# A four-layer graph network on one core: the change of layers in a written order, third passes two banks behind, projection pairs spread, longer first fills

## The chip, the cores and the metric

The kernel runs on one core of a Trainium2 chip. Times are device microseconds of one execution. A core has TensorE (PE in the profile, its weight loads apart as PEld), VectorE (DVE), ScalarE (ACT), GpSimd (POOL) and SyncE (SP), which here issues DMAs only. Each engine runs its own instructions in order and waits on semaphores for the others. The measure is the median of the runs, lower is better.

## The reference

The inputs are 1024 nodes of 512 features, 16384 edges, and a condition tensor of 16 batches of 256 rows by 512.

```python
def _attn(xf, cond, Wq, Wk, Wv, Wo):
    xb = xf.reshape(BS, n // BS, d)                      # 16 batches of 64 nodes
    q = (xb @ Wq).reshape(BS, -1, H, DH)                 # 8 heads of 64
    k = (cond @ Wk).reshape(BS, -1, H, DH)
    v = (cond @ Wv).reshape(BS, -1, H, DH)
    att = jnp.einsum('bnhd,bmhd->bhnm', q, k) * DH ** (-0.5)
    w = jax.nn.softmax(att, axis=-1)
    o = jnp.einsum('bhnm,bmhd->bnhd', w, v).reshape(BS, -1, H * DH)
    return (o @ Wo).reshape(n, d)
...
x_in = h_in
h = batch_norm(x_in)
h = _gcn(h, src, dst, gcn_in_w, gcn_in_b, n)             # normalised neighbour sums
for i in range(4):
    a = _attn(_ln(h, ln2_w[i], ln2_b[i]), cond, Wq[i], Wk[i], Wv[i], Wo[i])
    h = h + a
    u = _ln(h, ln3_w[i], ln3_b[i]) @ geglu_w[i] + geglu_b[i]
    val, gate = jnp.split(u, 2, axis=-1)
    h = h + (val * gelu(gate)) @ ffo_w[i] + ffo_b[i]
h = _gcn(h, src, dst, gcn_out_w, gcn_out_b, n)
return x + h + x_in                                       # x_in is relu(layernorm(x))
```

## The kernel before

The nodes are held as eight blocks of 128 rows (`h[0]` to `h[7]`, parts of the tile `hall`). All of the kernel is one traced function; a scheduler then orders each engine's instructions by dependencies and by the order of the trace, except where the code fixes it: `pin` chains PE's instructions in written order, `issue_after` holds an instruction behind another, `waiting_for` does so across engines. PSUM has eight banks of 128 x 512, all of one ring (`bank`), and large SBUF tiles come from a ring of 36 `slots`.

**The start.** The batch norm, the projection into the first graph step (`hw_in`) and the counting of edges (`cs`) come first; `begin` (L682) fills PE's pauses there with parts of layer 0's keys and values in plain float32 (one unit of eight matmuls of 128x512 records): `k0` while the batch norm's shift is awaited, `v0` after the counts, `k1` while the degrees' inverse root is worked out. Then the first aggregation runs over the blocks (`agg_in`), then layer 0's layer norm, keys, values and queries.

**Keys and values.** `Twelve` (L341) is one unit, a 128 x 512 output in one bank from operands split into twelve-bit parts: `begin` multiplies the high parts, then the low parts (four matmuls each, in the float form fp32r), and asks ACT to scale the bank (L359); `end` adds the third pass, sums times sums, and copies the bank out (ACT L366 for even units, DVE L364 for odd). The parts of the condition are `ah_c` (ACT L299), `al_c` (DVE L300), `as_c` (POOL L302); those of the weights `bh`, `bl`, `bs` (L310 to L320). For the value weights, `bs_wv` is made by ACT and POOL through an extra tile (`room`), for the key weights by DVE. `steps_of` runs units one behind the other: the third pass of a unit follows the first two of the next.

**The rounds.** In each layer, `g` runs over eight blocks (two batches each). Round `g` of 0 to 6 does: scores (`sc`, PE), softmax (maximum on DVE L810, exponentials on ACT L815, division on DVE L820), the four key units of block `g + 1`, transposes of the probabilities (`tr_pr`) and their product with the values (`po`, in `mix`), the four value units of block `g + 1`, and for odd `g` the output projection of two blocks (`attn_out_pair`, L895) as seven quarter products in two banks `oab` and `ocd`, with sums on POOL (`pair_sums`). The condition of block `g + 2` is split meanwhile (`split_cond`).

**The feed-forward** follows with gated quarters (`Quad`, `Gated`) and the products of `ffn_out` (L1182), in four banks `fa` to `fd`, whose results DVE adds into `kept` and `hall`.

**The change of layers** (L1680 to L1692, and the head of the next layer, L1381 to L1399): the last two `ffn_out` of a layer, each for half of the blocks; the split of the next layer's key weights, condition and value weights; sums of the query weights on POOL; the layer norm of each half (moments and a root by small DVE operations, `less`, the scaling of four blocks on ACT L1318), the transposes (`tr_ln`) with scaling into `ln2T`, and then keys and values of block 0, and queries (`qa` and so on). The first half's transposes come ahead of the keys.

## Time and profile before

| | |
|---|---|
| median of three runs | 2480.94 us (2479.92 to 2481.77) |
| profiled execution | 2480.42 us |
| its span | 2478.6 us |
| granted TensorE clock, mean | 0.991 |

The profile gives for each engine its busy time; a busy PE is one with a matmul in flight. Of ACT's work in the whole span, 112.1 us are gate functions, 118.1 us exponentials and some 146 us the scalings of key and value banks; POOL's largest group is `as_c`:

```profile
L302 POOL TENSOR_TENSOR as_c<-ah_c,al_c 128x512 fp32r<-128x512 f32 x128 | 189.3, 1506 | 543.8 <-DVE al_c L300 490.3
L1094 ACT ACTIVATE g<-g 128x512 f32<-128x512 f32 x192 | 112.1, 584 | 280.8 <-PE g L1080 278.5
L359 ACT ACTIVATE v<-v 128x512 f32<-128x512 f32 x127 | 73.9, 582 | 222.4 <-PE v L348 222.4
L359 ACT ACTIVATE k<-k 128x512 f32<-128x512 f32 x126 | 72.6, 590 | 141.0 <-PE k L348 141.0
L815 ACT ACTIVATE pr<-sc,nmax 128x256 f32<-128x256 f32 x256 | 118.1, 478 | 76.7 <-DVE nmax L810 76.6
```

A row of groups reads: line, engine, operation, what it writes from what, shapes, count | busy us, mean ns of one | idle us of the engine just before these, and what ended most of it. A row of the waits reads: engine, what waited, what it waited for: us in total, times, longest. A row of the timeline reads: start, us, engine, line, operation, count, and in brackets the engine's idle time before it with its releaser.

### The profile page before, as it was taken

The page shows a single profiled execution, that of the slowest core. Times are in us where ns is not written, and L with a number is a line of the kernel's source. Part 1 is how long each engine was busy: PE and PEld are TensorE (multiplying, and loading weights), DVE is VectorE, ACT ScalarE, POOL GpSimd, SP SyncE. Part 2 cuts the span into 40 slices and gives each one's busy share as a digit, 9 for nine tenths or more (in the row PEclk, how much of TensorE's full clock was granted, in tenths as well). Part 3 has the DMA queues.
Part 4 walks back from the last instruction along what each step waited for, and adds up shares of the span by engine and source line. Part 5 has one row for each costly group of instructions (what it writes and reads, how often), then busy time and mean ns, then how long its engine had stood idle before and what let it go on. Part 6 is the DMA issues. An engine that isn't in the chain of part 4 may idle for free. (4 is left out here: it accounts for less than half of the span.)

```text
span 2478.6 us, 33729 instructions
## 1 busy us (share of the span) xinstructions
PE 2384.1 (96%) x12532; PEld 1775.7 (72%) x12532; DVE 1586.5 (64%) x3053; ACT 998.1 (40%) x2023; POOL 949.6 (38%) x851
## 2 busy tenths in 40 slices
PE   8999999999989999999989999999989999999999
PEld 4667786577867777477766777577766777667787
DVE  9764455787675445777784444777785444678764
ACT  7434454343334445443333444533334444434320
POOL 0133222665332224455532223446532322366531
PEclk9999999999999999999999999999999999999999
DMA  6042120111301101011202111021121111011140
GB/s 195 21 134 82 47 86 18 43 43 51 107 20 54 56 18 52 22 56 48 90 29 65 47 35 35 18 60 52 43 90 47 47 40 47 18 43 43 51 145 35
DMA packets 108843, 138.31 MB, mean 56 GB/s; under 512 B 8232, under 2 KB 65904, under 8 KB 108672
## 3 DMA queue, kind: packets, MB, share of 16 engines
q1 hardware_dynamic: 106576, 130.64, 16.6%
q0 software_dynamic: 1376, 4.30, 0.5%
q8 instruction: 104, 1.70, 0.3%
q10 hardware_dynamic: 720, 1.11, 0.1%
q14 instruction: 67, 0.55, 0.1%
HBM read 119.25 MB, written 16.78 MB: 55 GB/s over the span
## 5 line engine op out<-in xcount | busy, mean ns | idle before, releaser
L302 POOL TENSOR_TENSOR as_c<-ah_c,al_c 128x512 fp32r<-128x512 f32 x128 | 189.3, 1506 | 543.8 <-DVE al_c L300 490.3
L1094 ACT ACTIVATE g<-g 128x512 f32<-128x512 f32 x192 | 112.1, 584 | 280.8 <-PE g L1080 278.5
L1031 POOL TENSOR_TENSOR gsa<-gha,gla 128x512 fp32r<-128x512 f32 x96 | 126.1, 1336 | 103.5 <-DVE gla L1028 103.5
L359 ACT ACTIVATE v<-v 128x512 f32<-128x512 f32 x127 | 73.9, 582 | 222.4 <-PE v L348 222.4
L348 PE MATMUL k<-as_c,bs_wk 128*128 128x512 f32 x504 | 141.8, 404 | 18.1 <-ACT k L359 18.1
L1031 POOL TENSOR_TENSOR gsb<-ghb,glb 128x512 fp32r<-128x512 f32 x48 | 70.0, 1458 | 219.4 <-DVE glb L1028 219.4
L815 ACT ACTIVATE pr<-sc,nmax 128x256 f32<-128x256 f32 x256 | 118.1, 478 | 76.7 <-DVE nmax L810 76.6
L348 PE MATMUL v<-bh_wv,ah_c 128*128 128x512 f32 x508 | 145.6, 408 | 0.0
L364 DVE COPY v<-v 128x512 f32<-128x512 f32 x62 | 42.3, 681 | 153.0 <-PE v L348 153.0
L348 PE MATMUL v<-bs_wv,as_c 128*128 128x512 f32 x508 | 139.8, 397 | 0.0
L348 PE MATMUL k<-ah_c,bh_wk 128*128 128x512 f32 x504 | 139.1, 399 | 0.0
L1195 PE MATMUL fa<-wff,fT 128*128 128x256 f32 x512 | 124.2, 385 | 13.6 <-DVE kept L1205 13.6
L1080 PE MATMUL g<-gr,gsa 128*128 128x512 f32 x384 | 136.6, 437 | 0.0
L348 PE MATMUL k<-al_c,bl_wk 128*128 128x512 f32 x504 | 136.5, 393 | 0.0
L348 PE MATMUL v<-bl_wv,al_c 128*128 128x512 f32 x508 | 136.3, 390 | 0.0
L1107 ACT ACTIVATE g<-g,gcols 128x512 f32<-128x512 f32 x96 | 67.5, 703 | 164.5 <-DVE g L1115 161.3
L359 ACT ACTIVATE k<-k 128x512 f32<-128x512 f32 x126 | 72.6, 590 | 141.0 <-PE k L348 141.0
L348 PEld LDWEIGHTS k<-as_c,bs_wk 128*128 128x128 f32 x504 | 90.2, 189 | 45.9 <-ACT k L359 13.3
L1080 PE MATMUL g<-gr,gha 128*128 128x512 f32 x384 | 122.8, 401 | 0.0
L1195 PEld LDWEIGHTS fa<-wff,fT 128*128 128x128 f32 x512 | 97.1, 191 | 35.2 <-DVE kept L1205 18.0
L1080 PE MATMUL g<-gl,gla 128*128 128x512 f32 x384 | 118.6, 390 | 0.0
L348 PEld LDWEIGHTS v<-bs_wv,as_c 128*128 128x128 f32 x508 | 92.9, 188 | 28.7 <-issue 9.2
(368 smaller groups left out, 5868.7 us busy)
## 6 DMA issues: line engine op xcount, KB each, us to landing
ct<-cond_dram SPq DMA_DIRECT2D x48, 512.0 KB, 4.5
wff<-in_L_gnn_ffo_w_dram SPq DMA_DIRECT2D x32, 512.0 KB, 4.5
gxb<-in_L_gnn_geglu_w_dram SPq DMA_DIRECT2D x96, 128.0 KB, 2.2
gxa<-in_L_gnn_geglu_w_dram SPq DMA_DIRECT2D x96, 128.0 KB, 2.4
cond<-in_L_gnn_cond_dram SPq DMA_DIRECT2D x32, 256.0 KB, 3.7
cond_dram<-ct SPq DMA_DIRECT2D x16, 512.0 KB, 3.7
wk<-in_L_gnn_Wk_dram SPq DMA_DIRECT2D x8, 512.0 KB, 6.1
wv<-in_L_gnn_Wv_dram SPq DMA_DIRECT2D x8, 512.0 KB, 8.4
```

The source lines that it names most:

```text
L302: nc.gpsimd.tensor_tensor(twelve_bits(s)[:, k, :], h[:, k, :], l[:, k, :], OP.subtract)
L348: pin(nc.tensor.matmul(self.bank, twelve_bits(left[k // 2])[:, k % 2, self.c * P:(self.c + 1) * P], twelve_bits(right[k // 2])[:, k % 2, : ...
L359: nc.scalar.mul(self.bank, self.bank, 1.0 + TINY)
L364: nc.vector.tensor_copy(self.to, self.bank)
L815: nc.scalar.activation(pr3[:, a, :], ps3[:, a, :], AF.Exp, bias=nmax[:, a:a + 1], accum_out=tot[:, a:a + 1])
L1031: pin(nc.gpsimd.tensor_tensor(s_at, h_at, l_at, OP.subtract))
L1080: pin(nc.tensor.matmul(to, self.part(i, which)[:, k, :], self.rights[i][which].bitcast(F32R)[:, k, :], start=start and k == 0, stop=stop a ...
L1094: pin(nc.scalar.mul(to, to, 1.0 + TINY))
L1107: pin(nc.scalar.activation(to, of, AF.Gelu, bias=gcols[:, cg:cg + 1]))
L1195: each(nc.tensor.matmul(to[:, q * M:(q + 1) * M], left[i][k][:, (2 * s + q) * P:(2 * s + q + 1) * P], right[i][:, k, :], start=start and q ...
```

## The change

- `staggered` takes the place of `steps_of`, and `keys` and `values` return lists of units. In the rounds, a key unit's third pass comes two units behind instead of one: k0, k1, k2, third of k0, k3, third of k1, third of k2, first transposes, third of k3.
- In a pair, quarter product 5 precedes 4; the third pass of the third value unit stands between the second and third part of the pair; the last product of a pair goes behind the next round's scores, except at `g` = 5. For odd `g`, the split of the condition goes behind the pair's sums. One layer norm of blocks moves from `g` = 5 to `g` = 6.
- At a change of layers PE's and DVE's orders are written out (`pin`, and the new `in_order`, which chains DVE's instructions in the order of the trace). The splits of weights and condition, the moments and the roots stand at chosen places of the two `ffn_out`. The transposes of the first half come behind the first two passes of the first value unit and the last key unit's third pass, those of the second half behind the last value unit. The sums of the value weights move to DVE, the query-weight sums behind the second `less`.
- At the start, two plain key units are made ahead of `hw_in`, the plain value unit is cut in two around the degrees, and layer 0 begins with keys ahead of transposes.

The core of the diff:

```diff
+    @contextmanager
+    def in_order(engine):
+        traced = nc.cur_bb.bb.instructions
+        n = len(traced)
+        before = next((i for i in reversed(traced) if i.engine == engine), None)
+        yield
+        for i in traced[n:]:
+            if i.engine == engine:
+                if before is not None:
+                    tc.add_manual_dep(i, before.name, mybir.DependencyInfo(
+                        mybir.DependencyClass.NoSync, mybir.DependencyReason.DATA))
+                before = i
...
-    def plain(to, left, c, right):
-        for k in range(KC):
+    def plain(to, left, c, right, of=range(KC)):
+        for k in of:
             nc.tensor.matmul(to, left[k // 2][:, k % 2, c * P:(c + 1) * P],
...
-    def steps_of(units):
-        before = None
-        for u in units:
+    def staggered(units, beside):
+        for i, u in enumerate(units):
             u.begin()
-            if before:
-                before.end()
-            before = u
-            yield
-        before.end()
-    def keys(l, g, wk, begun=None):
+            if i:
+                units[i - 1].end()
+            if i in beside:
+                beside[i]()
+        units[-1].end()
+    def keys(l, g, wk, begun=None, n=0):
         kTs[g] = begun or slots_of(2, f"kT_{l}_{g}")
-        return steps_of([Twelve(f"k_{l}_{g}_{c}", wk, c, conds[g], kTs[g][c // 2][:, c % 2, :], c % 2)
-                         for c in range(1 if begun else 0, KC)])
-    def values(l, g, wv, begun=None):
+        return [Twelve(f"k_{l}_{g}_{c}", wk, c, conds[g], kTs[g][c // 2][:, c % 2, :], c % 2)
+                for c in range(n, KC)]
+    def values(l, g, wv, begun=None, n=0):
         vs[g] = begun or slots_of(2, f"v_{l}_{g}")
-        return steps_of([Twelve(f"v_{l}_{g}_{c}", conds[g], c, wv, vs[g][c // 2][:, c % 2, :], c % 2)
-                         for c in range(1 if begun else 0, 2 * MB)])
+        return [Twelve(f"v_{l}_{g}_{c}", conds[g], c, wv, vs[g][c // 2][:, c % 2, :], c % 2)
+                for c in range(n, 2 * MB)]
...
     with tc.issue_after(shifted_last.ins):
-        begin("k0", raw_wk, raw_x[0, 0])
+        for c in range(2):
+            begin("k0", c, raw_wk, raw_x[0, 0])
...
-        begin("v0", raw_x[0, 0], raw_wv)
+        first_v = bank("begun_v0")
+        plain(first_v, raw_x[0, 0], 0, raw_wv, range(2))
         with tc.issue_after(load_dve.ins):
             for j in counted:
                 if j % 2:
                     degrees(j // 2, C[j // 2], t512(f"part_{j // 2}"))
+        with tc.issue_after(degrees.last.ins):
+            plain(first_v, raw_x[0, 0], 0, raw_wv, range(2, KC))
+        nc.scalar.copy(begun["v0"][0][:, 0, :], first_v)
...
-        product(4, d, False)
-        nc.vector.tensor_tensor(h22, d, h22, OP.add)
         product(5, b, False)
         nc.vector.tensor_tensor(u2, b, p1, OP.add)
         t.tensor_tensor(p7, p7, u2, OP.add)
+        product(4, d, False)
+        nc.vector.tensor_tensor(h22, d, h22, OP.add)
         t.tensor_tensor(h22, p7, h22, OP.add)
...
         if r:
             each(nc.vector.tensor_tensor(u, a, u, OP.add))
+            for do in beside[2:]:
+                do()
         else:
             nc.scalar.copy(u, a)
         product(6, c, True)
...
-        for do in beside[1:]:
+        for do in beside[1:2]:
...
+    mv_ready = {}
+    def take_moments(l, blocks):
+        n = len(blocks)
+        mv = mv_ready[blocks[0]] = small.tile([P, 2 * n], F32, tag=f"mv{n}", name=f"mv_{l}_{blocks[0]}",
+                                              bufs=2)
+        moments_into(mv, [h[nb] for nb in blocks], f"ln2_{l}_{blocks[0]}")
     def ready_first(l, blocks):
-        name = f"ln2_{l}_{blocks[0]}"
-        scaled_by_act(blocks, *moments([h[nb] for nb in blocks], name), name)
+        mv, name = mv_ready.pop(blocks[0]), f"ln2_{l}_{blocks[0]}"
+        scaled_by_act(blocks, mv, deviations(mv, name), name)
...
-    with waiting_for(scale_first.last, mybir.EngineType.Pool):
-        wq = load_w(Wq[0], "wq_0")
-        ffb = load_row(ffo_b, 0, "ffb_0")
-        wq = weight_sums(wq, "wqs_0")
+    wq = load_w(Wq[0], "wq_0")
+    ffb = load_row(ffo_b, 0, "ffb_0")
...
         if l:
-            flow = keys(l, 0, wk)
-            for _ in range(4):
-                next(flow)
-            then = values(l, 0, wv)
-            next(then)
-            next(flow, None)
-            ready_first(l, left_to_turn[2:])
+            units = keys(l, 0, wk) + values(l, 0, wv)
+            to_turn = [0, 1, 4, 5], [2, 3, 6, 7]
+        else:
+            scale_first(1, deviations(mv_first[1], "ln2_0_4"))
+            with waiting_for(scale_first.last, mybir.EngineType.Pool):
+                wq = weight_sums(wq, "wqs_0")
+            units = keys(0, 0, wk, begun["k0"], 2) + values(0, 0, wv, begun["v0"], 1)
+            to_turn = [0, 1, 2, 3], [4, 5, 6, 7]
+        def turn_some():
+            turn_first(l, to_turn[0])
+            if l:
+                sum_first(nc.gpsimd, 0)
+                sum_first(nc.gpsimd, 1)
+        staggered(units, {4 if l else 2: turn_some, len(units) - 1: lambda: turn_first(l, to_turn[1])})
+        if not l:
             sum_first(nc.gpsimd, 0)
             sum_first(nc.gpsimd, 1)
-            for _ in range(3):
-                next(then)
-            turn_first(l, left_to_turn)
-            sum_first(nc.vector, 2)
-            sum_first(nc.vector, 3)
-            next(then, None)
-        else:
-            scale_first(1, deviations(mv_first[1], "ln2_0_4"))
-            turn_first(0, [0, 1, 2, 3])
-            for _ in keys(0, 0, wk, begun["k0"]):
-                pass
-            turn_first(0, [4, 5, 6, 7])
-            for nb in range(2):
-                sum_first(nc.gpsimd, nb)
-            for nb in range(2, 4):
-                sum_first(nc.vector, nb)
-            for _ in values(0, 0, wv, begun["v0"]):
-                pass
             fetch_cond(2)
+        sum_first(nc.vector, 2)
+        sum_first(nc.vector, 3)
...
-        oTs, flow = [], None
+        oTs, ends = [], []
         for g in range(NG - 1):
             if g == NG - 2:
                 take_ln3()
                 raw = load_geglu(l, 0)
             probs = scores(l, g, qT, kTs.pop(g))
-            if flow:
-                next(flow, None)
+            for end in ends:
+                end()
+            if g == NG - 2:
+                ln3_norm(g - 2, g - 1)
...
-            flow = keys(l, g + 1, wk, begun.pop("k1") if l == 0 and g == 0 else None)
-            for _ in range(4):
-                next(flow, None)
-            then = values(l, g + 1, wv)
-            oTs.append(mix(l, g, probs, vs.pop(g), (lambda: next(flow, None), nothing,
-                                                    lambda: next(then))))
-            flow = then
+            k = keys(l, g + 1, wk, *((begun["k1"], 1) if l == 0 and g == 0 else ()))
+            for i, u in enumerate(k):
+                u.begin()
+                if i > 1:
+                    k[i - 2].end()
+            k[-2].end()
+            v = values(l, g + 1, wv)
+            oTs.append(mix(l, g, probs, vs.pop(g), (k[-1].end, nothing, v[0].begin)))
...
-            split_cond(l, g + 2)
+            with tc.issue_after(pair_sums.last.ins) if g % 2 else nullcontext():
+                split_cond(l, g + 2)
             if l:
                 load_cond(l, g + 3)
-            next(flow)
-            next(flow)
+            v[1].begin()
+            v[0].end()
+            v[2].begin()
+            v[1].end()
             if g % 2:
                 pair = attn_out_pair(g - 1, *blocks, wo7, bank(f"oab_{l}_{g}"), bank(f"ocd_{l}_{g}"),
                                      pin)
...
                                  f"ln3_{l}_{g - 3}")
             if g == NG - 2:
                 for nb in range(4):
-                    ln3_turn(nb)
-            next(flow)
+                    ln3_turn(nb, each=pin)
+            v[3].begin()
             if g % 2:
-                for _ in pair:
-                    pass
-            if g == NG - 3:
-                scale_kept()
-                ln3_norm(g - 1, g)
+                next(pair)
+            v[2].end()
+            ends = [v[3].end]
+            if g % 2:
+                next(pair)
+                if g == NG - 3:
+                    next(pair, None)
+                    scale_kept()
+                else:
+                    ends.insert(0, lambda pair=pair: next(pair, None))
             if g == NG - 2:
                 for nb in range(4, 6):
-                    ln3_turn(nb)
+                    ln3_turn(nb, each=pin)
                 for nb in (g - 2, g - 1):
                     ln3_sums(nc.gpsimd, nb)
...
-            ffn_out(l, R - 1, 0, fT, wff, kept)
-            wk = right_parts(raw_wk, f"wk_{l + 1}")
-            with waiting_for(Gated.last, mybir.EngineType.Pool):
+            wk, wv = [[], [], []], [[], [], []]
+            def split(to, raw, name, *of):
+                for i in of:
+                    for part, t in zip(to, right_parts(raw[i:i + 1], f"{name}_{l + 1}_{i}")):
+                        part.extend(t)
+            half = [0, 1, 4, 5], [2, 3, 6, 7]
+            with in_order(mybir.EngineType.DVE):
+                ffn_out(l, R - 1, 0, fT, wff, kept, pin, (lambda: split(wk, raw_wk, "wk", 0),
+                                                          lambda: split(wk, raw_wk, "wk", 1)))
+                take_moments(l + 1, half[0])
+                ffn_out(l, R - 1, 1, fT, wff, kept, pin, (lambda: split_cond(l + 1, 0),
+                                                          lambda: split(wv, raw_wv, "wv", 0, 1),
+                                                          lambda: ready_first(l + 1, half[0])))
+                take_moments(l + 1, half[1])
+                ready_first(l + 1, half[1])
+            with waiting_for(scaled_by_act.last, mybir.EngineType.Pool):
                 wq = weight_sums(wq, f"wqs_{l + 1}")
-            ready_first(l + 1, [0, 1, 4, 5])
-            split_cond(l + 1, 0)
-            ffn_out(l, R - 1, 1, fT, wff, kept)
-            wv = right_parts(raw_wv, f"wv_{l + 1}", acc_tile)
-            turn_first(l + 1, [0, 1, 4, 5])
-            left_to_turn = [2, 3, 6, 7]
-            ready_first(l + 1, left_to_turn[:2])
```

More of the change, by code (lines that the diff above doesn't have):

```diff
@@ L306, in right_parts @@
     def right_parts(x, name, room=None):
-        parts = [slots_of(2, f"{n}_{name}") for n in ("bh", "bl", "bs")]
+        parts = [slots_of(len(x), f"{n}_{name}") for n in ("bh", "bl", "bs")]
         for i, (h, l, s, x) in enumerate(zip(*parts, x)):
@@ L561, in degrees @@
         nc.vector.tensor_tensor(of_d, part[:, :P], part[:, P:2 * P], OP.add)
-        nc.tensor.matmul(pdeg[:, d:d + 1], of_d, ones, start=True, stop=True,
-                         skip_group_check=True)
+        degrees.last = nc.tensor.matmul(pdeg[:, d:d + 1], of_d, ones, start=True, stop=True,
+                                        skip_group_check=True)
     def low_hot(t, name):
@@ L680, in gnn_kernel, with begin @@
     begun = {n: slots_of(2, f"{n}_begun") for n in ("k0", "v0", "k1")}
-    def begin(n, left, right):
-        a = bank(f"begun_{n}")
-        plain(a, left, 0, right)
-        nc.scalar.copy(begun[n][0][:, 0, :], a)
+    def begin(n, c, left, right):
+        a = bank(f"begun_{n}_{c}")
+        plain(a, left, c, right)
+        nc.scalar.copy(begun[n][c // 2][:, c % 2, :], a)
     with tc.issue_after(shifted_last.ins):
-        begin("k0", raw_wk, raw_x[0, 0])
+        for c in range(2):
+            begin("k0", c, raw_wk, raw_x[0, 0])
     with ExitStack() as behind:
@@ L707, in gnn_kernel @@
     with waiting_for(rsqrt.first, mybir.EngineType.PE):
-        begin("k1", raw_wk, raw_x[0, 1])
+        begin("k1", 0, raw_wk, raw_x[0, 1])
     def of_twelve_bits(rows):
@@ L770, in acc_tile, with turn @@
         return accs.tile([P, 512], F32, tag="acc", name=name)
-    def turn(xn, to_halves, c0, wcol, bcol, name, by=(0, 1)):
-        pt = transposed(xn, name)
+    def turn(xn, to_halves, c0, wcol, bcol, name, by=(0, 1), each=lambda ins: ins):
+        pt = transposed(xn, name, each)
         for k in range(KC):
@@ L889, in pair_sums @@
         t.tensor_tensor(s2, s1, a11, OP.subtract)
-        t.tensor_tensor(s4, a12, s2, OP.subtract)
+        pair_sums.last = t.tensor_tensor(s4, a12, s2, OP.subtract)
         return [a11, a12, s4, a22, s1, s2, a21], more[:, M:], acc_tile(f"ou_{n}")
@@ L1313, in scaled_by_act @@
         less = small.tile([P, 4], F32, tag="less", name=f"less_{name}", bufs=1)[:, :n]
-        nc.vector.scalar_tensor_tensor(less, mv.rearrange("p (n c) -> p n c", c=2)[:, :, 0], -1.0,
+        scaled_by_act.last = nc.vector.scalar_tensor_tensor(less, mv.rearrange("p (n c) -> p n c", c=2)[:, :, 0], -1.0,
                                        root, OP.mult, OP.mult)
@@ L1328, in turn_first @@
             xn, c0 = xns.pop(nb), nb % 4 * P
-            turn(xn, lnT[nb // 4], c0, LN2W + l * KC, LN2B + l * KC, f"ln2_{l}_{nb}")
+            turn(xn, lnT[nb // 4], c0, LN2W + l * KC, LN2B + l * KC, f"ln2_{l}_{nb}", each=pin)
     nc.vector.tensor_scalar(cols[:, :2 * L * KC], cols[:, :2 * L * KC], DH ** -0.5, None, OP.mult)
@@ L1430, in ln3_norm, with ln3_turn @@
                     xns.update(zip(blocks, scaled(of, *moments(of, name), name)))
-        def ln3_turn(nb, by=(0, 1)):
+        def ln3_turn(nb, by=(0, 1), each=lambda ins: ins):
             turn(xns.pop(nb), ln3T[nb // 4], nb % 4 * P, LN3W + l * KC, LN3B + l * KC,
-                 f"ln3_{l}_{nb}", by)
+                 f"ln3_{l}_{nb}", by, each)
         def ln3_sums(t, nb):
@@ L1538, in gnn_kernel @@
         probs = scores(l, g, qT, kTs.pop(g))
-        next(flow, None)
+        for end in ends:
+            end()
         attn_out(l, g - 1, oT, wo)
```

## The prediction

> **What bounds the kernel now.** I read the page first, then TensorE's waits by cause, then stretches of the span.

> ```profile
> span 2478.6 us, 33729 instructions
> PE 2384.1 (96%) x12532; PEld 1775.7 (72%) x12532; DVE 1586.5 (64%) x3053; ACT 998.1 (40%) x2023; POOL 949.6 (38%) x851
> ```

> TensorE (PE) is busy 2384.1 of 2478.6 us, so 94.5 us are idle, and a change that only reorders work has these to win, plus what half clock costs. The other engines matter where PE waits for them. PE's waits:

> ```profile
> PE tr_ln L187 <- ACT xn_ln L1318: 20.3, 3, 7.3
> PE k L348 <- ACT k L359: 18.1, 22, 2.9
> PE fa L1195 <- DVE kept L1205: 13.6, 11, 2.3
> PE oab L282 <- DVE ou L912: 7.4, 12, 0.8
> PE ocd L282 <- DVE hall L919: 7.3, 12, 0.6
> ```

> Columns: total us, times, longest. The first row is the three changes of layers (second-half layer norm late); `k` is the third pass of a key unit, which reopens the bank that ACT has just scaled; `oab` and `ocd` are the projection pairs. The diff aims at all of these. The eight waits of `fa` inside the feed-forward stay.

> The three changes of layers by stretch, each from the end of the last covered product to the first queries matmul (the third row ends 0.46 late: its queries begin at 1885.54, so 46.52), then single windows by clock:

> ```profile
> 687.40:732.95 45.55, 35.58 (x152) 28.82 (x152) 33.67 (x78) 19.49 (x36) 17.16 (x16) 0.89 0.00 0
> 1263.06:1308.50 45.44, 34.37 (x153) 28.06 (x152) 33.56 (x78) 19.38 (x36) 17.15 (x16) 0.89 0.00 0
> 1839.02:1886.00 46.98, 34.88 (x154) 28.74 (x154) 34.10 (x79) 20.05 (x37) 17.12 (x16) 0.89 0.01 1
> 690.01:693.42 3.41, 3.41 (x9) 0.50 0.00 0
> 700.25:707.07 6.82, 4.60 (x19) 0.50 0.00 0
> 707.07:732.95 25.88, 23.84 (x110) 1.00 0.00 1
> 85.85:92.67 6.82, 6.18 (x8) 0.50 0.11 4
> 133.63:137.05 3.42, 3.42 (x10) 0.50 0.96 252
> ```

> Columns: length, then busy us of PE, PE's loads, DVE, ACT, POOL, and the granted clock (in the last five rows PE and the clock alone). PE works 34 to 36 of some 45 us. Half clock stretches busy time: in the first change (3.41 + 4.60)/2 = 4.0 us of the 35.58 are lost to it, so the work is some 31.5.

> **Part 1: the change of layers.** The diff puts the first transposes behind the key units, writes the DVE order out, moves the sums of the value weights (4 of 128x512 each time) from POOL to DVE, and the query-weight sums behind the second layer norm.

> ```profile
> 689.71 3.52 PE L1195 MATMUL fa<-wff,fT 128*128 128x256 f32 x8 [2.32 <-DVE kept L1205]
> 702.47 3.67 PE L187 MATMUL tr_ln<-ident,xn_ln 128*128 128x128 f32 x16 [5.63 <-ACT xn_ln L1318]
> L313 DVE SCALAR_TENSOR_TENSOR bl_wv<-wv,bh_wv 128x512 fp32r<-128x512 f32 x4 | 2.6, 682 | 0.0
> L300 DVE SCALAR_TENSOR_TENSOR al_c<-ah_c,ct 128x1024 fp32r<-128x1024 f32 x3 | 3.7, 1217 | 0.5 <-ACT ah_c L299 0.5
> L302 POOL TENSOR_TENSOR as_c<-ah_c,al_c 128x512 fp32r<-128x512 f32 x4 | 5.9, 1495 | 14.4 <-DVE a_ln L142 14.4
> 802.61 6.02 POOL L302 TENSOR_TENSOR as_c<-ah_c,al_c 128x512 fp32r<-128x512 f32 x4 [22.42 <-DVE al_c L300]
> 802.99 2.00 DVE L300 SCALAR_TENSOR_TENSOR al_c<-ah_c,ct 128x1024 fp32r<-128x1024 f32 x1
> L1318 ACT ACTIVATE xn_ln<-hall,less_ln,y_ln 128x512 f32<-128x512 f32 x8 | 6.1, 806 | 31.5 <-DVE less_ln L1314 31.5
> L299 ACT ACTIVATE ah_c<-ct 128x1024 fp32r<-128x1024 f32 x1 | 1.1, 1057 | 0.0
> 718.09 0.16 DVE L146 SCALAR_TENSOR_TENSOR y_ln<-b_ln,y_ln 128x2 f32<-128x2 f32 x1
> 718.29 0.16 DVE L142 SCALAR_TENSOR_TENSOR a_ln<-y_ln,v_ln 128x2 f32<-128x2 f32 x1
> ```

> In the timeline of a quiet stretch, `al_c` on DVE took 2.00 against 1.217, while four `as_c` ran on POOL: operations of the two engines that read two tiles take turns, and one `as_c` with a DVE operation between costs about 1.25 + 0.6 = 1.85. (1.25 is an estimate for a free one: 6.02 for four, less the 0.78 by which `al_c` was held and about 0.2.) On the clock of the first change I walk the new order by hand:
> - `kept` of the second half is reached about 0.9 earlier, since half of the key-weight splits fill DVE's wait ahead of it: PE's gap is 1.45 for 2.32.
> - The deviations (12 dependent tiny operations at the 0.20 pitch of the two rows at 718, 2.4) now come in one run; the adds that free PE's banks stand behind them: a new gap of 1.2 at `fc`.
> - `less` is ready at 691.1; ACT's four layer-norm scalings (6.1/8 = 0.76 each, 3.0) and the second `ah_c` (1.06) end at 695.1; DVE's two `al_c` (1.2 each) stand behind the adds of `fc`, `fd` and `kept` and end at 697.1. Keys start at 695.3 and wait 0.5 for `al_c`. What is queued behind `ah_c` on ACT is the value-weight split and the first key scale; PE waits for both.
> - The first third pass needs all four `as_c`. They start at 697.1 and alternate with the eight value-weight operations on DVE: 697.1 + 1.3 + 3 x 1.87 = 704.0. PE has had two units' plain passes by 699.9 and idles 4.05: the largest new wait.
> - The rest of the value split (0.68 each), two adds, four norms and twelve tiny operations bring the second `less` to 714.1. DVE's copy of a key bank stands behind it, and a transpose waits 1.0 for that bank; ACT's copy stands behind the second four scalings, and the second value unit waits 2.4.

> Idle: 1.45 + 1.2 + 0.5 + 4.05 + 1.0 + 2.4 = 10.6 (before: 45.55 - 35.58 = 10.0). Work: 24 products of 0.216 (5.2; eight take 1.73 in the feed-forward's timeline), 24 passes of 0.907 (21.8; the key rows below), 32 transposes (3.6), some 0.6 for changes between the two float forms: 31.2. Sum 41.8. Of half-clock windows I keep one for each change, where the 4.05 lies, at 3.41/2 = 1.7: 43.5. Against 45.55, 45.44 and 46.52 that gives 2.05 + 1.94 + 3.02, so **-7**. Bounds: no lock and no half clock -34 (rivals), a lock of twice the length +11.

> [...]

> **Part 2: third passes two banks behind, pairs spread** (28 rounds, 12 pairs).

> ```profile
> 828.62 1.08 ACT L359 ACTIVATE k<-k 128x512 f32<-128x512 f32 x2
> 829.26 1.19 PE L348 MATMUL k<-as_c,bs_wk 128*128 128x512 f32 x4 [0.61 <-ACT k L359]
> 832.12 1.07 PE L348 MATMUL k<-as_c,bs_wk 128*128 128x512 f32 x4
> 833.02 1.07 PE L348 MATMUL k<-ah_c,bh_wk 128*128 128x512 f32 x4
> 812.66 1.27 PE L348 MATMUL v<-bh_wv,ah_c 128*128 128x512 f32 x4
> 818.28 1.13 PE L282 MATMUL oab<-wo,oT 128*128 128x256 f32 x4 [0.81 <-DVE ou L912]
> 820.88 1.10 PE L282 MATMUL ocd<-wo,om 128*128 128x256 f32 x4 [0.61 <-DVE hall L919]
> ```

> ACT's first two key scales stand behind the eight exponentials (828.62); PE came at 828.65 and waited 0.61. In the new order a third unit's two passes (1.8) lie ahead of this third pass, which covers it. The softmax (last probabilities by 830.1, from the same timeline) is wanted by PE at 835.75 and, 0.61 earlier, at 835.1: still hidden. In the pairs, product 5 now comes ahead of 4 and a value third pass (0.91) between: the sum behind `oab` (0.42 on DVE, ending 0.81 late) is covered. The last product moves behind the next scores, except in one of three pairs of a layer: eight of twelve `ocd` waits go. The `k` row holds 18.1; less 2.9 in the prologue and 1.85 + 1.26 + 2.46 in the changes of layers, 9.6 lie in the rounds. Possible: 9.6 + 7.4 + 7.3 x 8/12 = 21.9. Costs: a block entered from the other float form takes 1.27 (812.66) for 1.07 (832.12), 0.2; I take 1.5 more of these in each pair, 12 x 0.3 = 3.6; and one short wait in a layer where the bank is scaled late stays, 4 x 0.35 = 1.4. **-17** (from -22 to -6, if each of the 28 rounds keeps 0.4 and each pair has 0.2 more). POOL's sums of a pair now go ahead of the next `as_c`; those are wanted a round later.

> **Part 3: longer first fills.**

> ```profile
> 19.81 3.60 PE L335 MATMUL begun_k<-ct,wk 128*128 128x512 f32 x8
> 26.54 1.12 PE L526 MATMUL hw_in<-w_in,h0T 128*128 128x512 f32 x2 [3.13 <-ACT h0T L518]
> 28.97 1.57 ACT L574 ACTIVATE off<-ids,minus_low 128x128 bf16<-128x128 f16 x5
> 32.04 0.83 PE L602 MATMUL cs<-hot,off 128*128 128x384 bf16 x7
> 86.18 0.17 DVE L137 TENSOR_SCALAR v_deg<-deg 128x8 f32<-128x8 f32 x1 [3.94 <-PEq L703]
> 123.81 2.02 PE L187 MATMUL tr_ln<-ident,xn_ln 128*128 128x128 f32 x16 [1.06 <-DVE xn_ln L175]
> 132.37 1.17 PE L348 MATMUL k<-as_c,bs_wk 128*128 128x512 f32 x4 [2.90 <-ACT k L359]
> ```

> A second plain key unit (3.43 pitch) fills the 3.13 and spares three passes (2.72) later. It ends 0.3 past 26.54, and its copy on ACT (0.59) pushes the `off` group and so the counts at 32.04; the half clock around 28 to 31 goes (1.6 of busy time), of which I credit 0.6, for `off` is then late: -2.72 + 0.3 - 0.6 = -3.0. The value unit is cut in two, so the degrees come 1.7 earlier; but `v_deg` waits for PE's sequencer at a branch (3.94, the row at 86.18), which now stands behind the second half. I take -1.5: half of the half-clock loss (6.18/2 = 3.1) of 85.85; bounds +0.6 and -4.6. In layer 0 the keys now start on the heels of the aggregation, ahead of the transposes: 1.06 + 2.90 and the half clock of 133.63 (1.71) go, 5.7, less 1.0 for queries that wait for sums which now all come at the end: -4.7. Sum **-9.2** (-3 to -13).

> **Sum.** -7 - 17 - 9.2 = -33.2 on the profiled execution of 2480.42 (span 2478.6 and 1.8 around it): **2447 us**. The median of the runs, 2480.94, is 0.5 above that execution. The feed-forward and the end keep their order and cost.

> **Rivals.**
> [...]
> - No lock: `as_c` at 1.25 beside a running DVE. The 4.05 goes, `less` comes 3.4 earlier and with it the 1.0 and 2.4, and no half clock: 34.4 each, -34: 2420. Against: 2.00 for 1.217.
> - The lock holds longer: 2.4 on each `as_c` (as 6.02/4 + 0.9): +2 at the first third pass, +2 at the second layer norm, a second half-clock window: 43.5 + 5.7 = 49.2, +11: 2465.
> - The rounds give only 6, as bounded above: 2458; the first fills nothing: 2456. The last is also the case that an edit doesn't do what it says, since the branch would hold everything where it is.
> - **Slower:** half clock over most of a change of layers. The new order has six gaps (1.45, 1.2, 0.5, 4.05, 1.0, 2.4) spread over some 42 us, or 12 windows of 3.41; if gaps of about a microsecond were enough to lower the clock, 10 of the 12 would run at half, 9 more than I count, each 1.7: 3 x 9 x 1.7 = +46, 2493. It decides from 33.2/(3 x 1.7) = 6.5 more windows in each change. For: 2.32 was enough at 690. Against: 1.85 at 710 (PE's gap ahead of a key's third pass there) left the clock at 1.00 after 707.

> **How the numbers follow.** My sum 0.48 (2440 to 2454); no half clock 0.16; no lock 0.07; longer lock 0.12; rounds or fills lost 0.09; slower 0.08. Changes within 0.2% (5 us) can't be told from none. Faster 0.88, same 0.04, slower 0.08. The range leaves out the slower case and most of the lock-free one: 2428 to 2466.

> **What would show it.** In the changed kernel's waits, `oab` gone, `ocd` at a third, `k` in the rounds below 2 us in all; at the changes of layers no `tr_ln` wait of 5 to 7 us, but a wait of about 4 for `as_c` ahead of the first third pass and 2 to 3 at the second value unit, and 42 to 44 us from the last product to the queries. Granted clock 1.00 around 28 to 31 and 134. I am wrong if key passes still wait in the rounds, if `as_c` takes about 1.25 next to the value split, or if the aggregation's start moves later.

## The result, and the profile after

| | before | changed |
|---|---|---|
| median | 2480.43 us (4 runs) | 2452.21 us (4 runs, 2452.06 to 2452.32) |
| ratio | | 0.9887 (95%: 0.987 to 0.9904) |
| profiled execution, its span | 2480.42, 2478.6 | 2452.32, 2450.5 |
| granted clock | 0.991 | 0.994 |

The forecast was 2447, within 2428 to 2466. The time is inside and the sign is right, but the sum hides errors that cancel: a cost of 27.5 us that it does not have, and gains that came out some 22 us larger than its terms. The page of the changed kernel, then its waits of TensorE:

```profile
span 2450.5 us, 33701 instructions
PE 2374.2 (97%) x12528; PEld 1777.1 (73%) x12528; DVE 1606.8 (66%) x3028; ACT 992.8 (41%) x2011; POOL 937.2 (38%) x839
```
```profile
PE po L856 <- DVE pT L870: 19.4, 4, 4.9
PE fa L1213 <- DVE kept L1223: 11.8, 11, 1.7
PE k L362 <- POOL as_c L316: 7.0, 6, 1.2
PE v L362 <- ACT kT L380: 5.7, 3, 2.2
PE ocd L296 <- DVE hall L937: 2.4, 4, 0.6
PE tr_ln L201 <- DVE kT L378: 1.5, 2, 0.8
PE k L362 <- DVE al_c L314: 1.2, 3, 0.4
```

`tr_ln` behind ACT (20.3), `k` behind ACT (18.1) and `oab` (7.4) are gone, `ocd` is at a third. On top stands a wait that the prediction does not have: `po`, the product of probabilities and values, waits 4.85 us for DVE's copy of the probabilities' transpose, once in each layer.

Stages by the timeline's first rows of the aggregation (`agg_in`), the queries (`qa`) and the gate products (`gc`), in us, four layers or three changes summed:

| stage | before | changed | difference | forecast |
|---|---|---|---|---|
| start to aggregation | 92.67 | 88.56 | -4.1 | |
| aggregation to queries | 55.99 | 47.09 | -8.9 | -9.2 with the row above |
| queries to gate products (the rounds), 4 | 1133.8 | 1128.8 | -5.0 | -17 |
| gate products to the next queries, 3 | 884.3 | 874.2 | -10.1 | -7 |
| last gate products to the end | 311.9 | 311.9 | 0 | 0 |

So the start and the changes of layers gave more than forecast, and the rounds 12 us less. Round 6 of layer 0 shows why. DVE and POOL, timeline of the changed kernel:

```profile
363.68 0.17 DVE L153 TENSOR_SCALAR y_ln<-v_ln 128x2 int32<-128x2 int32 x1
363.88 2.24 DVE L156 SCALAR_TENSOR_TENSOR a_ln<-y_ln,v_ln 128x2 f32<-128x2 f32 x1
366.15 0.16 DVE L158 TENSOR_TENSOR b_ln<-a_ln,y_ln 128x2 f32<-128x2 f32 x1
366.35 2.25 DVE L160 SCALAR_TENSOR_TENSOR y_ln<-b_ln,y_ln 128x2 f32<-128x2 f32 x1
368.63 2.31 DVE L156 SCALAR_TENSOR_TENSOR a_ln<-y_ln,v_ln 128x2 f32<-128x2 f32 x1
371.17 2.19 DVE L160 SCALAR_TENSOR_TENSOR y_ln<-b_ln,y_ln 128x2 f32<-128x2 f32 x1
375.50 0.68 DVE L870 COPY pT<-tr_pr 128x512 f32<-128x512 f32 x1
```
```profile
363.70 2.40 POOL L238 TENSOR_TENSOR ges<-wgate,wgate 128x1024 f32<-128x1024 f32 x1 [6.98 <-DVE v_ln L151]
366.18 2.40 POOL L239 TENSOR_TENSOR wgate<-wval,wgate 128x1024 f32<-128x1024 f32 x1
368.54 2.38 POOL L240 TENSOR_TENSOR ges<-ges,wval 128x1024 f32<-128x1024 f32 x1
371.00 2.35 POOL L241 TENSOR_TENSOR ges<-wval,ges 128x1024 f32<-128x1024 f32 x1
```

The layer norm of blocks 4 and 5, which the change moved behind round 6's scores, now runs at the same time as POOL's four sums of the gate weights. Four of six operations in a row on 2 elements a partition take 2.2 to 2.3 us, each until the end of the POOL operation that it meets. In the kernel before, POOL's sums began 3 us behind the end of this norm, and the same operations took 0.16 (DVE and POOL there):

```profile
383.08 0.16 DVE L142 SCALAR_TENSOR_TENSOR a_ln<-y_ln,v_ln 128x2 f32<-128x2 f32 x1
383.47 0.16 DVE L146 SCALAR_TENSOR_TENSOR y_ln<-b_ln,y_ln 128x2 f32<-128x2 f32 x1
388.29 2.39 POOL L224 TENSOR_TENSOR ges<-wgate,wgate 128x1024 f32<-128x1024 f32 x1 [10.15 <-DVE pr L820]
```

In the changed kernel the copy that PE needs starts at 375.50. PE's row, and the clock of the stretch behind it (length, PE busy, clock):

```profile
376.24 1.97 PE L856 MATMUL po<-pT,v 128*64 128x64 f32 x30 [4.83 <-DVE pT L870]
364.00:371.10 7.10, 7.10 (x41) 1.00 0.01 2
371.10:385.00 13.90, 9.07 (x82) 0.75 0.06 11
```

The clock of 0.75 over 13.9 us is half clock in half of it: it was 0.50 from 374.96 to 381.79.

### The profile page after: what moved, and what is told of

Read it like the earlier page. It is cut to its first block, busy times and chain, and to the rows that moved or that the text cites. A ratio compares the mean times of both kernels' runs of the same rounds, so it can differ in the third digit from the quotient of the medians.

```text
span 2450.5 us, 33701 instructions
## 1 busy us (share of the span) xinstructions
PE 2374.2 (97%) x12528; PEld 1777.1 (73%) x12528; DVE 1606.8 (66%) x3028; ACT 992.8 (41%) x2011; POOL 937.2 (38%) x839
## 3 DMA queue, kind: packets, MB, share of 16 engines
q10 hardware_dynamic: 720, 1.11, 0.1%
## 5 line engine op out<-in xcount | busy, mean ns | idle before, releaser
L362 PE MATMUL k<-as_c,bs_wk 128*128 128x512 f32 x500 | 135.8, 400 | 7.2 <-POOL as_c L316 7.0
L905 POOL TENSOR_TENSOR os<-oT 128x256 f32<-128x256 f32 x12 | 8.8, 734 | 318.8 <-DVE oT L879 318.8
```

What stands on the lines that cost most here:

```text
L362: pin(nc.tensor.matmul(self.bank, twelve_bits(left[k // 2])[:, k % 2, self.c * P:(self.c + 1) * P], twelve_bits(right[k // 2])[:, k % 2, : ...
L905: t.tensor_tensor(s1, a21, a22, OP.add)
```

## The experiments

**Is it the moved norm?** The norm of blocks 4 and 5 back to the end of round 5, ahead of the scores:

```diff
-            if g == NG - 2:
-                ln3_norm(g - 2, g - 1)
...
                     next(pair, None)
                     scale_kept()
+                    ln3_norm(g - 1, g)
```

> The layer norm of blocks 4 and 5 stands ahead of round 6's scores again, as before the change; all else is as changed. My theory: in round 6 it met POOL's four weight sums (2.4 us each), which hold DVE's small operations, and so held the copies of the probabilities' transposes: PE waited 4.85 us in each layer (19.4) and half clock followed. Then the four waits go and with them some 1 to 2 us of half clock a layer: 2428 us, 2424 to 2434. Rival: round 6 is bound by DVE's amount of work there, and the wait only moves to the transposes or the keys: 2445 to 2452.

Measured 2422.53 us (ratio to before 0.9772, 0.9756 to 0.9789), clock 0.999. The `po` wait is gone, and of waits in the rounds only `ocd` (2.4) and one key wait of 0.62 are left. The rounds took 1101.3, 32.4 less than before the change. So the moved norm cost the rounds 27.5: 19.4 of waits, and some 8 in which PE was busy longer for the same work, in part at half clock.

**The lock, or the norm's place on DVE?** By the lock I mean what the rows show: operations of DVE that read two tiles were held while one of POOL ran (2.2 to 2.3 us for 0.16 above, 2.00 for 1.217 in the row that the prediction quotes). The norm stays behind the scores; POOL's sums wait for its end:

```diff
-                with waiting_for(scores.last, mybir.EngineType.Pool):
+                with waiting_for(scaled.last, mybir.EngineType.Pool):
                     left = geglu_weights(l, 0, *raw)
```

> The layer norm stays behind round 6's scores as in the changed kernel, but POOL's weight sums wait for the end of that norm instead of the end of the softmax. If the lock is the cause, the small operations run at their 0.2 pitch, the norm ends some 8 us earlier, ahead of the transposes, and the 19.4 us of waits go: 2426 to 2434 us. If the place of the norm on DVE (12 small operations and two scalings, about 3.4 us, ahead of the copies) is the cause, the waits stay in part: above 2440 us.

Measured 2423.43 us in one run. DVE's and POOL's timeline in this run:

```profile
363.97 0.16 DVE L156 SCALAR_TENSOR_TENSOR a_ln<-y_ln,v_ln 128x2 f32<-128x2 f32 x1
364.17 0.16 DVE L158 TENSOR_TENSOR b_ln<-a_ln,y_ln 128x2 f32<-128x2 f32 x1
365.73 1.00 DVE L189 TENSOR_SCALAR xn_ln<-hall,mv_ln,y_ln 128x512 f32<-128x512 f32 x2
366.87 2.38 POOL L238 TENSOR_TENSOR ges<-wgate,wgate 128x1024 f32<-128x1024 f32 x1 [10.07 <-DVE xn_ln L189]
369.45 0.69 DVE L870 COPY pT<-tr_pr 128x512 f32<-128x512 f32 x1 [1.10 <-PE tr_pr L201]
```

The same operations at the same place run at a pitch of 0.2, and the copy waits for PE (1.10) instead of PE for the copy. The place on DVE was harmless; the meeting with POOL was the cost. That POOL's sums end 3 us later costs nothing that can be seen.

**What do the third passes and the pairs give?** Each put back alone in the changed kernel, first the third passes:

```diff
-                if i > 1:
-                    k[i - 2].end()
-            k[-2].end()
+                if i:
+                    k[i - 1].end()
```

> The changed kernel with the third pass of a key unit one unit behind in the rounds, as before the change. By my sum the key waits return, 0.35 to 1 us three or so times in a layer, 9.6 us in all: 2461 us (2458 to 2463). Rival: without these waits the rounds are bound by something else that PE meets later, and the reordering gives at most 3 us: 2452 to 2455.

Measured 2462.05 us in one run, +9.8; the rounds are 7.5 longer, and the other 2.3 lie in the changes of layers, which the edit does not touch. The total is as forecast, but not for the reason given: eight key waits came back (7.6 us), while the `po` wait shrank from 19.4 to 15.5, since PE came later to it. Next the pairs, product 4 again ahead of 5, and all of the pair ahead of the scores:

```diff
             v[3].begin()
-            if g % 2:
-                next(pair)
             v[2].end()
...
             if g % 2:
-                next(pair)
...
+                for _ in pair:
+                    pass
```

> The changed kernel with the projection pairs as before: product 4 ahead of 5, the value third pass ahead of the second part, the last product ahead of the scores. By my sum 7.4 us of waits for the sum behind oab and 4.9 for the sums behind ocd return, less 3.6 of changes between the float forms: 2461 us (2459 to 2464). Rival: the changes of form eat the gain: 2450 to 2455.

Measured 2470.02 us in one run, +17.8, twice the forecast. The waits of this run:

```profile
PE ocd L296 <- DVE hall L937: 7.3, 12, 0.6
PE oab L296 <- DVE ou L930: 7.1, 12, 0.8
```

They returned as counted (7.1 and 7.3 - 2.4: 12.0 in 20 waits), and the rounds are 18.4 longer, so each wait cost 0.32 more than its row says. The timeline of the kernel before shows where it hides, beside the row with the 0.61 wait that the prediction quotes:

```profile
827.58 1.07 PE L348 MATMUL k<-al_c,bl_wk 128*128 128x512 f32 x4
830.29 1.08 PE L348 MATMUL k<-ah_c,bh_wk 128*128 128x512 f32 x4
```

From 827.58 the next pass would start 0.907 later; it started at 829.26, 0.77 late, not 0.61; and the pass behind it at 830.29, another 0.12 late: 0.89 in all. The rest of the error, 3.6, is the charge for changes of float form. In the changed kernel:

```profile
283.08 1.02 PE L296 MATMUL oab<-wo_sums,os 128*128 128x256 f32 x4
283.94 1.03 PE L296 MATMUL ocd<-wo_sums,os 128*128 128x256 f32 x4
284.61 1.27 PE L362 MATMUL v<-bs_wv,as_c 128*128 128x512 f32 x4
285.72 1.03 PE L296 MATMUL oab<-wo,oT 128*128 128x256 f32 x4
```

The value pass takes 1.11 to the next start instead of 0.91, but the `ocd` ahead of it 0.67 instead of 0.86: the 0.2 that I charged is given back by the block before. In these rows the change of form costs nothing.

**The same without the norm in the way.** The kernel of the first run (2422.53), third passes one behind, same diff as above:

> The kernel with the norm back, and the third passes of the rounds one unit behind as before the change. The rounds are 32.4 us shorter than before without the moved norm, and pairs put together cost 17.8; if the two are all, this one costs 14.6: 2437 us (2435 to 2438). That is the 9.6 us of waits in the profile and 0.28 more for each of some 18, since a matmul after a wait takes 0.1 to 0.3 longer to the next. Rival: the gap in the profile is the whole price: 2432.

Measured 2432.48 us in one run. Of these 9.9, 2.0 are half clock ahead of the aggregation (0.87 from 82 to 95 for 1.00), which has nothing to do with the edit. The rounds are 8.5 longer, and the trace has eight key waits behind ACT again, two in each layer:

```profile
PE k L362 <- ACT k L373: 6.1, 8, 2.1
```

The rounds of the kernel before have sixteen, 9.2 us, not the eighteen that I took: in rounds 0, 2, 4 and 6 of each layer. Here they lie in rounds 0 and 6; rounds 2 and 4, where a pair's last product now stands behind the scores, have none. So my 14.6 fell, and the rival is right only in the number: the kernel with the norm back has one key wait of 0.62 itself, so 5.5 us of waits were put back, and (8.5 - 5.5)/7 = 0.43 a wait lie above the rows. With pairs spread, the last product behind the scores already covers half of the key waits, so the two edits share them. Of the 0.1 to 0.3 that I took for a matmul after a wait, the rows show the lower end: in the kernel before, a third pass behind such a wait took 0.99 to 1.04 to the next start at full clock, for 0.91.

**The changes of layers.** The changed kernel there: PE's waits in the second one (timeline), POOL and DVE in the first, and the three stretches (length, PE, PE's loads, DVE, ACT, POOL, clock):

```profile
1259.30 0.51 PE L362 MATMUL k<-as_c,bs_wk 128*128 128x512 f32 x1 [1.17 <-POOL as_c L316]
1274.58 1.20 PE L362 MATMUL v<-bh_wv,ah_c 128*128 128x512 f32 x4 [2.18 <-ACT kT L380]
682.41 7.18 POOL L316 TENSOR_TENSOR as_c<-ah_c,al_c 128x512 fp32r<-128x512 f32 x4 [37.53 <-DVE al_c L314]
685.14 1.67 DVE L334 SCALAR_TENSOR_TENSOR bs_wv<-bh_wv,bl_wv 128x512 fp32r<-128x512 f32 x1
673.32:715.43 42.11, 35.44 (x152) 27.67 (x153) 31.16 (x69) 20.20 (x36) 17.97 (x16) 0.92 0.00 0
1244.64:1287.38 42.74, 34.42 (x154) 26.73 (x153) 31.07 (x69) 20.41 (x36) 17.93 (x16) 0.96 0.00 0
1817.57:1858.68 41.11, 32.81 (x152) 25.59 (x152) 31.05 (x69) 20.29 (x36) 17.95 (x16) 1.00 0.00 0
```

In the kernel with the norm back, PE gets two more passes ahead of the first third pass there (two units behind), against the `as_c` waits:

```diff
-        staggered(units, {...})
+        staggered(units, {...}, 2 if l else 1)
```

> The kernel with the norm back (2422.5 us), and at the changes of layers the third passes two units behind as in the rounds, so that PE has two more passes (1.8 us) ahead of the first third pass, which waits twice 1.17 us for as_c there. My theory: DVE's chain (splits, second norm, less), then ACT's scalings, set when the second value unit can start; PE then only waits longer there: 2421 to 2423 us. Rival: each wait costs by itself, as PE's own row shows: the 7.0 us of as_c waits go: 2415 to 2417.

Measured 2428.95 us: slower by 6.4, which neither theory had. The waits of this run:

```profile
PE tr_ln L201 <- DVE kT L378: 10.5, 3, 3.5
PE v L362 <- ACT kT L380: 5.3, 3, 1.9
PE k L362 <- POOL as_c L316: 3.5, 3, 1.2
```

Half of the `as_c` wait went, but the transposes wait 3.5 a change for DVE's copy of a key bank, which stands behind the second `less`, and the second value unit starts at 695.78 in the first change, against 695.58 with one behind. So PE's two more passes did not bring that start forward, which fits my theory that the order of DVE and ACT sets it. What I missed comes behind it: the last key unit's third pass (0.9), now deferred past that start, and half clock behind the 3.5 gap (the first two passes of the unit took 1.87 and 1.71 to the next start for 0.91, some 1.7 together; clock 0.92 over the change): 2.6 of the 2.3 to 2.7 that each change lost. If that order binds, moving ACT's key copies ahead of the scalings that wait for `less` must help (`scale_later` is called behind the third key unit's copy):

```diff
+    def scale_later():
+        with tc.issue_after(Twelve.last.ins):
+            to_scale.pop()()
...
-                ready_first(l + 1, half[1])
+                ready_first(l + 1, half[1], to_scale)
```

> The kernel with the norm back, and at the changes of layers ACT's copies of the first and third key unit ahead of its second four layer-norm scalings, which wait for the second less. The second value unit waits for the first of these copies 2.2 us a change (5.4 in all). If that copy alone holds it, 2.2 to 2.4 go at each change: 2416 us (2414 to 2418). Rival: PE then only meets the next thing of the same chain (the transposes of the second half, whose scalings now end 1.0 later, or the bank that DVE copies behind less): 2420 to 2423.

Measured 2415.74 us (2413.62 to 2417.97; ratio 0.9737, 0.9721 to 0.9753): 6.8 less than with the norm back. The `v` and `tr_ln` waits are gone; only `as_c` (7.0) and `al_c` (1.2) are left of this list. Then both together, with DVE's copy of the second key unit also ahead of the second norm's root:

```diff
-                take_moments(l + 1, half[1])
-                ready_first(l + 1, half[1], to_scale)
...
+        staggered(units, {2: lambda: take_moments(l, to_turn[1]), 3: normalise_second,
+                          4: scale_and_turn, ...}, 2 if l else 1)
```

> The kernel with the copies first (2415.7 us), and at the changes of layers the third passes two units behind, with DVE's copy of the second key unit ahead of the second norm's root. If the chain that DVE's and ACT's order makes was what gave 5.2 us a change back in the run with two units behind, the 7.0 us of as_c waits now go and most of the time with them: 2408 to 2412 us. If DVE's chain to the second less binds by itself, the second half's transposes wait instead: 2415 to 2420.

Measured **2406.03 us** (2405.36 to 2407.73; ratio 0.9707, 0.969 to 0.9723), clock 1.000: the best of the study, 1.9% below the changed kernel, and below its forecast, although 3.5 us of `as_c` waits are left. Its first change of layers, below that of the kernel with the norm back:

```profile
665.62:706.72 41.10, 32.74 (x153) 25.61 (x153) 31.10 (x69) 20.27 (x36) 17.94 (x16) 1.00 0.00 0
666.04:703.00 36.96, 32.81 (x155) 26.27 (x156) 31.55 (x73) 20.36 (x38) 16.96 (x16) 1.00 0.00 0
```

The second window runs 0.96 past the first queries matmul, at 702.04, so the change takes 36.00 for 41.10. In the profiled executions the three changes are 11.0 us shorter than with the copies first: 3.5 are `as_c` waits, and most of the rest is half clock. I estimate it at 6.8 there, from clocks of 0.96, 0.96 and 0.92 over 42 to 43 us each; here the clock is 1.000.

The last part of that change, the value weights' sums, given back to ACT and POOL (in the kernel with the norm back):

```diff
-right_parts(raw[i:i + 1], f"{name}_{l + 1}_{i}")
+right_parts(raw[i:i + 1], f"{name}_{l + 1}_{i}", acc_tile if name == "wv" else None)
```

> The kernel with the norm back, with the sums of the value weights at the changes of layers made by ACT and POOL again, as before the change. By the chain (DVE's value split, norm, less, ACT's scalings, key copies) DVE is four operations of 0.68 shorter, so the second value unit could start up to 2.7 earlier, but POOL's four more sums (1.25 each) hold DVE's norm operations, and ACT has four more of 0.62: 2420 to 2426 us. If the lock rules, as in round 6, the small operations wait 1.2 each and it is slower: 2428 to 2436.

Measured 2420.72 us (2419.95 to 2421.5) in two runs, no slower than with DVE: 1.8 less is under the 5 us that the prediction takes as the least that can be told from none, and in the profiles the changes of layers take 871.4 for 871.5. The value unit's wait fell from 5.4 to 3.9, which fits a shorter chain on DVE. Moving these sums to DVE gave nothing that can be seen.

**The start.** The value unit whole, ahead of the degrees, as before:

```diff
-        plain(first_v, raw_x[0, 0], 0, raw_wv, range(2))
+        plain(first_v, raw_x[0, 0], 0, raw_wv)
...
-        with tc.issue_after(degrees.last.ins):
-            plain(first_v, raw_x[0, 0], 0, raw_wv, range(2, KC))
```

> The kernel with the norm back, with the plain value unit of the start whole and ahead of the degrees, as before the change. In the trace the aggregation started 4.1 us earlier than before, 0.8 of which were there before the degrees; so the cut is worth 3.3 if half clock around 86 to 92 goes with it: 2426 us (2425 to 2427). Rival (my sum): 1.5, 2424.

Measured 2429.21 us in one run, but 5.3 of the 6.7 lie in the stages of the last two changes of layers (293.1 and 293.3 for 290.4 and 290.6), with a clock of 0.92 and 0.93 for 0.96 and 0.96, which the edit does not touch. The aggregation began at 90.53, against 88.49; in the run with the norm back and third passes one behind, which has the cut, it began at 90.53 too, with the clock at 0.87 from 82 to 95 in both. So the cut shows no price apart from whether half clock is granted. In the other ten profiles with the cut the aggregation began at 88.4 to 88.9; one profile without it, and the kernel before, can't show whether the cut is what spares half clock, and this stays open. Layer 0's transposes ahead of its keys, as before:

```diff
-        staggered(units, {2: turn_some, len(units) - 1: ...})
+            turn_some()
+            staggered(units[:2], {})
+            turn_first(l, to_turn[1])
+            staggered(units[2:], {})
```

> The kernel with the norm back (2422.5 us), with layer 0's transposes ahead of its keys and of its values, as before the change; the two plain key units at the start stay. From the aggregation to the queries the trace went from 55.99 to 47.09, of which 2.72 are three passes fewer; so the order is worth 6.2: 2429 us (2427 to 2430). My sum had 4.7: 2427. Rival: the waits for the transposes are covered anyway once fewer keys come after them: 2423.

Measured 2424.73 us (2424.24 to 2425.22), +2.2, near the rival. From the aggregation to the queries it took 49.42 for 47.07, with one wait of 1.8 for `xn_ln`. So of the 8.9 the order gave 2.35 and the spared passes 2.72. The other 3.8 are left by difference: they are near the key wait of 2.90 and its half clock, which this run, with one unit fewer to run, no longer shows either, but no run puts that unit back.

## Why the prediction was right or wrong

- **Part 2, the rounds, is where it failed.** Forecast -17 with bounds of -22 and -6; measured -5.0, outside them. Two of its steps were wrong, in opposite directions. First, the step "the softmax ... still hidden" covered the probabilities, but the layer norm that moved from round 5 to round 6 was not priced at all, nor what it runs beside: +27.5, shown by the two runs that take the meeting away. Second, "Possible: 21.9 ... Costs: 3.6" was mis-sized: without the norm the rounds give -32.4, 15.4 more. The 3.6 for changes of form and most of the 1.4 for short waits were not there (one of 0.62 is left). The other 10.5 are more than the rows hold. These hold 21.5, since two key waits of 0.18 that lie in the changes of layers were counted into the rounds, and each of these 36 waits cost about 0.3 beyond its row (0.32 and 0.43 in the two runs that put waits back). Why a wait costs more than its row is not shown.
- **Part 1, the changes of layers**, forecast 43.5 us each: measured 42.11, 42.74 and 41.11. The walk held in order and nearly in size: 1.7, 0.85, 0.4, 2 x 1.17, 0.8 and 2.2 in the second change, for 1.45, 1.2, 0.5, 4.05, 1.0 and 2.4. The term that was mis-sized is the `as_c` wait: the third pass does not need all four at once. Its first two matmuls ran ahead of the wait, and the other two waited 1.17 each for a piece of their own. The alternation is as forecast: 7.18 for four, and the four DVE operations beside it took 1.18 to 1.75 each for 0.68. The half clock, 3.41 us of it each in my sum, came as 6.82 us (688.99 to 695.81), 3.41 (1276.08 to 1279.49) and none. Where it came it cost less than that: in the first change PE was busy 2.7 longer than in the run with the norm back (35.44 for 32.74), but the change took only 1.0 longer (42.11 for 41.10), since PE then waited less behind it (1.31 for 2.17 at the second value unit, none for 0.81 at the transposes).
- **Part 3, the start**, forecast -9.2: measured -13.0, at the upper bound. The half clock of 85 to 93 went whole in that execution (clock 1.00 from 82 to 95, for 0.74 before) where I took half of it. The order of layer 0 was worth less than my 4.7 (2.35), and the spared unit, by difference, more.
- **The rivals.** The longer lock came true in a place I had not looked at: not on `as_c`, but on the small operations of round 6 (its own sum is 3 x 49.2 - 137.5 = +10, not +11). The rival of rounds that give only 6 has nearly the measured number, -5.0, but by another cause. The slower case did not come: no change of layers had more than 6.82 us of half clock. The case without half clock, 0.16 in the forecast, came in the third change alone, at 41.11. For the clock itself the rows say: 0.50 from 374.96 on, in a gap of 4.83 that began at 371.41; and in the first change, with the same two gaps of 1.17, 0.92 in the changed kernel and 1.00 in the one with the norm back. Behind the same gaps it was 1.00 in the second (1257 to 1276) and third change of the changed kernel; behind the gap of 2.18 in the second it fell to 0.50, behind one of 2.17 in the third it stayed at 1.00. Which gaps lower it is not shown.

## What to carry to other kernels

When an edit moves work of a helper engine, list what the other engines run at the new place: here eleven operations that took 2.1 us in all behind each other (second run) took 10.5 beside four of POOL's of 2.4. Price a wait from start to start of the instructions around it, not by its idle row, and price edits that cover the same waits together. Where an engine's order holds a bank's release behind an operation that waits for something late, put the release first; that gave 6.8 us here, where giving the waiting engine more work cost 6.4.
